# The pool of the large buffer allocated ahead of the constants

## The chip, the core and the metric

The kernel runs on one core of a Trainium2 chip. The metric is the time of one execution on the device, in microseconds, and the median over several executions is what counts. A NeuronCore has a matrix engine (TensorE, PE in the profile, with its weight loads shown apart as PEld), a vector engine (VectorE, DVE), a scalar engine (ScalarE, ACT), a general engine (GpSimd, POOL) and a queue engine (SyncE, SP). Its working memory, SBUF, has 128 partitions; a tile has the same byte address in each of them. The results of matrix products go to another memory, PSUM, in banks of 512 float32 values per partition.

## What is computed

Two graph layers over 4096 nodes with 512 features each, both with a dense 4096 x 4096 adjacency matrix and a layer norm over the sum with their input:

```python
# layer 0
xw = relu(sign(x)) @ sign(w0).T
x1 = layernorm(x + relu(adj @ xw))
# layer 1
node_att = softmax(x1 @ node_w, axis=0)
h = x1 @ edge_w
e = where(adj > 0, h @ h.T, -9e15)
edge_att = softmax(e, axis=1)
out = layernorm(x1 + adj * (node_att * edge_att) @ (x1 @ w1) + bias)
```

All inputs and the output are float32.

## The kernel before

The nodes are handled in 32 blocks of 128 (the partitions) and in 8 groups of 512 (one PSUM bank). The kernel passes through these stages, and TensorE works in all of them:

1. *Signs.* `whole(g)` (L177) loads a part of x transposed, turns it into signs on VectorE and multiplies by the signs of w0 (`bw`). Its result, rows of `xw`, is written by VectorE (L222) and ScalarE. `follow(g)` (L240) multiplies two early row blocks of the adjacency by the rows of `xw` that are there (L246, L247).
2. *First aggregation, adj @ xw.* The loop over `n` (L343 on) takes the other 30 row blocks. For each it loads the block of the transposed adjacency in two halves (`at`, 1 MB each, L358, three buffers), and treats each half in two quarters of 8 column blocks. ScalarE rounds a quarter to the format float32r (`hi`, L363), VectorE takes the difference (`lo`, L365), each with two buffers, and TensorE multiplies hi and lo by the same row of `xw`, adding into one bank (L373, L374): 16 matmuls for a quarter, 64 for a block. hi and lo are the stationary operands (loaded by PEld, 128 x 128), the row `xw[:, kb, :]` of 512 values is the moving operand. Between the quarters VectorE carries the residual, layer norm and node weights of an earlier block (`rest`, L290 on), and the mask of the second layer is made ahead (`premask`, L271 on: a load on the ACT queue, one VectorE instruction, a store on the POOL queue). At each block's end TensorE does four transposes (L333).
3. *h.* `seven` (L90) multiplies with seven products in place of eight; the result is `hT`.
4. *h h^T*, with the masks and row minima (`Single`, `Couple`, L641 and L714), and
5. *the second aggregation and the last product* (`Sums`, L1081, and `Finish`, L1208), with running sums in `sums` and with `w1_s` behind them.

`xw`, `hT` and `over` (of which `sums` and `w1_s` are parts) are one after the other in one buffer of 65,536 bytes per partition: the pool `big`, with one buffer of the tag "large". `xw` and `bw` are float32r, as are hi, lo and `ba`, the signs of x; all other operands of the large products are float32.

The allocator places pools one behind the other in the order in which they are entered, each tile at a multiple of 32 bytes. Ahead of everything stand 16,512 bytes (129 x 128) that the runtime and four small constants use. Before, `const` comes next: `ident` (512 bytes at 16,512), `eps`, `shift`, `node_s`, `nmax`, `gmax`, `node_att`, `nsum` and `gsum`, together 960 bytes. So the large buffer begins at 17,472, which is 136 x 128 + 64. `rows`, `small` and all later pools follow; nearly all their tiles are a multiple of 128 bytes long, so the tiles that hold 512 bytes or more (`at`, `hi`, `lo`, `bw`, `ba`, `warm`, `x1T`, `lent`, `slot`, `lop`, ...) begin at a multiple of 128 plus 64 too. A row of `xw` has 2,048 bytes, so each row of it begins 64 bytes after a multiple of 128.

The lines around the moving operand, and those that allocate it:

```python
    const = ctx.enter_context(tc.tile_pool(name="const", bufs=1))
    big = ctx.enter_context(tc.tile_pool(name="big", bufs=1))
...
    xw = big.tile([P, NB, D], F32R, name="xw", tag="large")
...
                            nc.tensor.matmul(acc, hi[:, c, :], xw[:, kb, :], start=(kb == 0), stop=False)
                            nc.tensor.matmul(acc, lo[:, c, :], xw[:, kb, :], start=False, stop=(kb == NB - 1))
```

Of the kernel before, what the change touches and what calls it, by code (L numbers as in the profile page):

```python
# [29 lines left out]
def kernel(  # L30
# [22 lines left out]
    HD = D // 2  # L53
    QC = HB // 2

    const = ctx.enter_context(tc.tile_pool(name="const", bufs=1))
    big = ctx.enter_context(tc.tile_pool(name="big", bufs=1))
    rows = ctx.enter_context(tc.tile_pool(name="rows", bufs=4))
    small = ctx.enter_context(tc.tile_pool(name="small", bufs=2))
    dram = ctx.enter_context(tc.tile_pool(name="dram", bufs=1, space=bass.MemoryType.DRAM))  # L60
# [98 lines left out]
    with (  # L159
# [110 lines left out]
        bufs = deque([pair[:, 0, :], pair[:, 1, :], single, ends])  # L270
# [1186 lines left out]
```

## Time and profile before

| | |
|---|---|
| median of 5 executions | 1938.6 us (1936.35 to 1938.7) |
| the profiled execution | 1937.62 us |
| its span, first to last instruction | 1935.6 us |
| TensorE's mean granted clock in it | 0.999 of full speed |
| DMA traffic | 508.72 MB, 263 GB/s in the mean |

A row of a group of instructions in the profile has the line, the engine, the operation, the tiles it writes and reads, the shape, the count, then the time in which at least one of the group was busy, the mean duration of one in ns, and the idle time of the engine ahead of them with what ended it. A matmul's duration is counted until its last result, and its end is modelled; matmuls follow one another before the one ahead has ended. How fast they really pass is therefore read from their starts, in the view of instructions in order of time, whose columns are the start in us, the duration in us, engine, line, operation and tiles.

### The profile page before, as it was taken

The page shows a single profiled execution, that of the slowest core. Times are in us where ns is not written, and L with a number is a line of the kernel's source. Part 1 is how long each engine was busy: PE and PEld are TensorE (multiplying, and loading weights), DVE is VectorE, ACT ScalarE, POOL GpSimd, SP SyncE. Part 2 cuts the span into 40 slices and gives each one's busy share as a digit, 9 for nine tenths or more (in the row PEclk, how much of TensorE's full clock was granted, in tenths as well). Part 3 has the DMA queues.
Part 4 walks back from the last instruction along what each step waited for, and adds up shares of the span by engine and source line. Part 5 has one row for each costly group of instructions (what it writes and reads, how often), then busy time and mean ns, then how long its engine had stood idle before and what let it go on. Part 6 is the DMA issues. An engine that isn't in the chain of part 4 may idle for free.

```text
span 1935.6 us, 20238 instructions
## 1 busy us (share of the span) xinstructions
PE 1917.9 (99%) x6742; PEld 1203.5 (62%) x6742; DVE 1389.4 (72%) x2062; ACT 1022.4 (53%) x1614; POOL 291.8 (15%) x413
## 2 busy tenths in 40 slices
PE   9999999999999999999999999999999999999998
PEld 6888888888644445454555444456666666666655
DVE  7766676676765567566664996687869987798747
ACT  5433333333202567576677665546766576757731
POOL 0122122222341101011111111111111110111100
PEclk9999999999999999999999999999999999999999
DMA  8888888887475478577773998777778787877731
GB/s 310 294 325 311 297 317 309 325 311 284 160 266 220 157 259 313 187 276 252 291 309 104 347 343 292 255 273 257 267 263 293 255 274 262 293 274 260 275 109 44
DMA packets 169527, 508.72 MB, mean 263 GB/s; under 512 B 15696, under 2 KB 41040, under 8 KB 161744
## 3 DMA queue, kind: packets, MB, share of 16 engines
q1 hardware_dynamic: 89472, 226.39, 34.9%
q0 software_dynamic: 64688, 239.10, 32.8%
q10 hardware_dynamic: 15264, 41.95, 5.9%
q8 instruction: 53, 0.87, 0.2%
q14 instruction: 50, 0.41, 0.1%
HBM read 385.74 MB, written 121.63 MB: 262 GB/s over the span
## 4 chain that ended last, share of the span: by engine, by line
PE 80%; DVE 10%; issue 4%; DMA 4%; ACT 1%; POOL 0%; POOLq 0%; DVEq 0%; SPq 0%
PE bank L1081 25%; PE seven L714 14%; PE acc L374 11%; PE acc L373 11%; PE pe L641 6%; PE seven L101 4%; PE po L1208 3%; PE pt L603 2%; DVE lent L847 1%; DMA slot<-s_d 1%; DMA lent<-s_d 1%; PE pw L214 1%; PE acc L246 1%; DVE lent L835 1%; PE pt L333 1%
## 5 line engine op out<-in xcount | busy, mean ns | idle before, releaser
L1081 PE MATMUL bank<-lent,lop 128*128 128x512 f32 (+1 forms) x1136 | 420.0, 517 | 0.0
L373 PE MATMUL acc<-xw,hi 128*128 128x512 f32 x960 | 376.4, 392 | 0.0
L374 PE MATMUL acc<-xw,lo 128*128 128x512 f32 x960 | 374.2, 390 | 0.0
L1081 PE MATMUL bank<-slot,lop 128*128 128x256 f32 (+1 forms) x1052 | 356.1, 486 | 1.5 <-DVE slot L862 1.5
L1081 PEld LDWEIGHTS bank<-lent,lop 128*128 128x128 f32 x1136 | 215.7, 190 | 173.9 <-issue 159.0
L1081 PEld LDWEIGHTS bank<-slot,lop 128*128 128x128 f32 x1052 | 199.6, 190 | 135.2 <-issue 116.9
L363 ACT CAST hi<-at 128x1024 fp32r<-128x1024 f32 x120 | 126.4, 1054 | 203.4 <-PE acc L373 148.4
L365 DVE TENSOR_TENSOR lo<-at,hi 128x1024 fp32r<-128x1024 f32 x120 | 146.9, 1224 | 85.0 <-ACT hi L363 85.0
L374 PEld LDWEIGHTS acc<-xw,lo 128*128 128x128 f32 x960 | 180.4, 188 | 37.1 <-DVE lo L365 0.3
L373 PEld LDWEIGHTS acc<-xw,hi 128*128 128x128 f32 x960 | 180.3, 188 | 36.7
L1090 ACT COPY over<-bank 128x512 f32<-128x512 f32 x200 | 114.5, 581 | 108.4 <-PE bank L1081 97.1
L641 PE MATMUL pe<-hT 128*128 128x512 f32 (+3 forms) x384 | 132.1, 486 | 0.0
L574 ACT ACTIVATE line<-line,nmax_c 128x512 f32<-128x512 f32 x160 | 114.8, 725 | 22.5 <-DVE nmax_c L565 22.3
L565 DVE CUSTOM_DVE_ANT_0 line<-lent,slot 128x512 f32<-128x512 bf16 x140 | 90.7, 689 | 48.4 <-ACT slot L651 26.7
L835 DVE CUSTOM_DVE_ANT_1 lent<-lent,line 128x2048 f32<-128x2048 f32 x40 | 91.4, 2286 | 22.6 <-DMA lent<-s_d 13.0
L841 ACT ACTIVATE slot<-slot 128x2048 f32<-128x2048 f32 x36 | 68.9, 1913 | 71.3 <-DMA slot<-in_adj_t_dram 65.4
L838 ACT ACTIVATE lent<-lent 128x2048 f32<-128x2048 f32 x40 | 76.5, 1912 | 54.7 <-DVE lent L835 54.6
L641 PEld LDWEIGHTS pe<-hT 128*128 128x128 f32 x384 | 64.6, 191 | 41.4 <-issue 33.8
L714 PE MATMUL seven<-hT 128*128 128x512 f32 x192 | 89.8, 593 | 0.0
L1053 ACT COPY bank<-over 128x512 f32<-128x512 f32 x144 | 84.9, 596 | 3.0 <-DVE left L973 0.2
L603 PEld LDWEIGHTS pt<-ident,lent 128*128 128x128 f32 x418 | 52.3, 141 | 52.1 <-issue 38.8
L604 ACT COPY slot<-pt 128x512 f32<-128x512 f32 (+3 forms) x123 | 68.4, 559 | 24.0 <-PE pt L603 24.0
(262 smaller groups left out, 2850.7 us busy)
## 6 DMA issues: line engine op xcount, KB each, us to landing
at<-in_adj_t_dram SPq DMA_DIRECT2D x60, 1024.0 KB, 6.8
lop<-lop_d SPq DMA_DIRECT2D x79, 512.0 KB, 4.9
lent<-s_d POOLq DMA_DIRECT2D x39, 1024.0 KB, 7.4
slot<-in_adj_t_dram POOLq DMA_DIRECT2D x38, 1024.0 KB, 7.4
s_d<-slot POOLq DMA_DIRECT2D x30, 1024.0 KB, 6.8
lent<-in_adj_t_dram POOLq DMA_DIRECT2D x26, 1024.0 KB, 7.5
lop<-lop_d SPq DMA_DIRECT2D x99, 256.0 KB, 4.2
lent<-in_adj_dram SPq DMA_DIRECT2D x48, 512.0 KB, 5.7
```

The costliest lines, as they stand in the source:

```text
L363: nc.scalar.copy(hi, aq)
L365: nc.vector.tensor_sub(lo, aq, hi.bitcast(F32))
L373: nc.tensor.matmul(acc, hi[:, c, :], xw[:, kb, :], start=(kb == 0), stop=False)
L374: nc.tensor.matmul(acc, lo[:, c, :], xw[:, kb, :], start=False, stop=(kb == NB - 1))
L565: nc.vector.tensor_tensor_reduce(line, mask, src, -1.0, HUGE, ALU.add, ALU.min, accum_out=nmax_c[:, b, c : c + 1])
L574: nc.scalar.activation(line, line, AF.Exp, bias=nmax_c[:, b, c : c + 1], scale=-1.0, accum_out=sum_c[:, b, c : c + 1])
L603: nc.tensor.transpose(pt[:, j, :], src[:, ts(j, P)], ident)
L641: nc.tensor.matmul(pe[:, lo * P :], hT[:, k, ts(A * BG + i, P)], hT[:, k, (B * BG + lo) * P : (B + 1) * W], start=(k == 0), stop=(k == KD ...
L714: nc.tensor.matmul(ps, left[m][:, k, q, :], right[m][:, k, :], start=(first and k == 0), stop=(k == KD // 2 - 1), skip_group_check=not first,)
L835: pinned[0](nc.vector._custom_dve(TENSOR_ADD_SAT, out=q, in0=q, in1=m, s0=0.0, s1=-HUGE))
L1081: nc.tensor.matmul(ps, lop[:, k, :], rop[:, k, :], start=start, stop=(k == K - 1), skip_group_check=True)
L1090: nc.scalar.copy(self.to(), self.bank[:, : self.w])
```

## The change

The two lines that enter the pools `const` and `big` change places:

```diff
+    big = ctx.enter_context(tc.tile_pool(name="big", bufs=1))
     const = ctx.enter_context(tc.tile_pool(name="const", bufs=1))
-    big = ctx.enter_context(tc.tile_pool(name="big", bufs=1))
     rows = ctx.enter_context(tc.tile_pool(name="rows", bufs=4))
```

In the built program the large buffer (`xw`, `hT`, `over`) then begins at 16,512, a multiple of 128, and the constants stand behind it: `ident` at 82,048 in place of 16,512, both multiples of 128, and the others likewise 65,536 bytes further up. The two pools together are as long as before, so every other tile keeps its address. The instructions of each engine and their order are the same: 3001 rows on TensorE, 2015 on VectorE, 1488 on ScalarE, 389 on GpSimd and 372 on SyncE in both programs.

## The prediction

> **What bounds the kernel now.** I read first the page's chain that ended last, then the busy time by stage, then the starts of single matmuls, and last who waits for whom.
>
> ```profile
> PE 80%; DVE 10%; issue 4%; DMA 4%; ACT 1%; POOL 0%; POOLq 0%; DVEq 0%; SPq 0%
> ...
> L373 PE MATMUL acc<-xw,hi 128*128 128x512 f32 x960 | 376.4, 392 | 0.0
> L374 PE MATMUL acc<-xw,lo 128*128 128x512 f32 x960 | 374.2, 390 | 0.0
> ```
>
> TensorE carries 80% of the chain, and the two groups that read `xw` as moving operand have no idle time ahead of them. They are the first aggregation. The stretches (PE, PEld, DVE, ACT, POOL busy, clock, DMA share, GB/s) show it from 57 to 507 us:
>
> ```profile
> 57.30:507.30 450.00, 449.97 (x2042) 372.29 (x2041) 312.45 (x481) 147.40 (x181) 107.62 (x151) 1.00 0.84 304
> ```
>
> TensorE is busy throughout, VectorE for 312.5 of 450 us (69%), the DMA engines for 84%. So the stage lasts as long as its matmuls, and the question is whether one of them can pass faster. The order of time says how fast they pass. In the middle of a block (start, duration):
>
> ```profile
> 199.63 0.39 PE L373 MATMUL acc<-xw,hi 128*128 128x512 f32 x1
> ...
> 206.89 0.39 PE L373 MATMUL acc<-xw,hi 128*128 128x512 f32 x1
> ```
>
> Between these two starts lie 32 matmuls: 7.26 us / 32 = 226.9 ns each; between most starts of the stage it is 226 or 227 ns. Now a float32 product of 256 columns in the second aggregation, and one of 128 columns, both read the same way:
>
> ```profile
> 1445.72 1.03 PE L1081 MATMUL bank<-slot,lop 128*128 128x256 f32 x4
> 1446.58 1.03 PE L1081 MATMUL bank<-lent,lop 128*128 128x256 f32 x4
> ```
>
> 0.86 us / 4 = 215 ns; over longer runs of starts 215.8. For 128 columns of float32 (the transposes at L603) starts are 109 ns apart. The difference, 106.8 ns for 128 columns, is 0.834 ns a column; with 512 columns of float32 at 429 ns (L1081) the same slope holds: 429 - 215.8 = 213.2 for 256. A float32 column therefore costs 0.833 ns and an instruction some 2.5 ns more. The float32r matmuls take 512 columns in 226.7, so they pass a column in half that, 0.417 ns: 512 x 0.4167 = 213.3, plus 2.5 is 215.8. They miss this by 10.9 ns. In the signs stage the matmuls `bw` x `ba` at L214, float32r too, run at 226 to 227 as well, while a bf16 matmul of 512 columns between two of its kind (L200, from 8.6 us on) is followed by the next after 215 or 216.
>
> The last view, what TensorE waited for in the whole run, has seven entries and these lead (us, times, longest):
>
> ```profile
> PE po L1208 <- DVE xb L1219: 4.3, 6, 1.4
> PE bank L1081 <- DVE slot L862: 1.5, 1, 1.5
> PE seven L101 <- DVE hT L122: 1.3, 1, 1.3
> PE acc L246 <- DVE xw L222: 1.3, 4, 0.6
> ```
>
> None lies in the aggregation. Next to nothing there waits, yet each matmul takes 5% longer than its columns.
>
> **What the Trainium skill says.** *TensorE: Matmul & The Clock Gate*, section "Back-to-back issue gap", gives N / 2.4 + 2.5 ns for an isolated matmul of N columns: 215.8 for 512. The bf16 and two-pass float32 spacings agree (215 to 216 and 429); the float32r spacing of 226.7 doesn't. *SBUF — State Buffer*, "Specifications (TRN2)", gives lines of 16 bytes; both addresses of `xw`, 17,472 and 16,512, are multiples of 16, so by that page nothing changes. Its section "Operand start alignment" is about legality and says that it timed nothing. No page prices a start 64 past a multiple of 128.
>
> **The change part by part.** It removes and adds no instruction and no wait, and moves none past another: the order on each engine, the queues of SP and POOL included, is the same. Only addresses differ. Three things are touched.
>
> *The moving operand of float32r.* The excess is 226.7 - 213.3 = 13.3 ns, or 13.3 / 0.4167 = 32 columns. Thirty-two float32 values are 128 bytes. A row of `xw` has 2,048 bytes: begun at a multiple of 128 it covers 16 pieces of 128 bytes, begun 64 later it touches 17. 17 / 16 x 213.3 = 226.67, and 226 and 227 in the ratio one to two is what the starts show. I infer that the operand is fetched by pieces of 128 bytes, each taking the time of 32 columns, so that a stream of one column per 0.417 ns is held up by the seventeenth; float32 in two passes and bf16 need half the bytes in a given time and don't notice it. That also says why they run at 215.8 and 429 although their operands begin at 64 as well. No matmul before reads float32r from a multiple of 128, so the aligned cost is bounded: above by 226.7 (no gain, unless the alignment itself did harm, for which no view speaks), below by 213.3. I take 215.8, the spacing of the other single-pass matmuls. Gain 10.9 ns.
>
> Main stage: 30 blocks x 64 = 1920 matmuls x 10.9 = 20.9 us. Some 210 of them, just behind the transposes and elsewhere, run at 228 to 236 and 29 at 313 to 319; what holds them I can't see. If these 240 gained nothing, 2.6 us would be lost; I take a third of it, 0.9. Signs stage: 128 matmuls at L246 and L247 x 10.9 = 1.4 us, but there TensorE also waits for VectorE's rows of `xw`, so part of the gain becomes wait; I take 0.6. The 64 at L214 read `bw`, which stays at 64, and gain nothing. Sum: 20.9 - 0.9 + 0.6 = 20.6 us.
>
> *Cover in the stage.* A quarter shrinks from 16 x 226.7 = 3.63 us to 3.45. hi and lo of a quarter are made while the one before is multiplied: 1.05 us on ScalarE (L363) and 1.22 on VectorE (L365), begun when TensorE gives a buffer back. In the steady blocks lo is ready 0.89 to 2.0 us before its first matmul; this lead falls by about 0.17 us and doesn't end. It is what comes next: it would decide if a quarter went below some 2.7 us. Once, at 492 us, lo was late already (0.3 us of wait); there I expect up to 0.2 us more. Transfers: the 84% of DMA time becomes 88%, 304 GB/s about 319. Single slices of a fortieth of this stage move up to 395. The queue of SP waits for buffers, not for bandwidth: 174 us for lo to free `at` (L358), and `at` lands 6.5 us after its issue (9.9 at most) while its three buffers cover 22.5 us, afterwards 21.6. TensorE's weight loads take 188 ns each beside the matmul; at a spacing of 215.8 such loads, of 190 ns, already keep up (L1081, 256 columns). Cover gone would return at most what was gained.
>
> *hT, sums, w1_s and the constants.* Their matmuls are float32 at 429 and 216, without the excess, so nothing is to be had. VectorE and ScalarE read and write them at 0 in place of 64. No instruction of the trace touches a large tile at a multiple of 128, apart from `ident`, whose own start stays one, so this is unmeasured; by the nearest row (L1090, 581 ns for 512 values, some 6 ns, one part in a hundred, up or down) for each, a bound that I set without a row that shows it, on engines with 72% and 53% of the span. I take nothing.
>
> After 507 us the chain is led by TensorE and by waits that begin with its own work (the largest, 1.3 us at 575, hangs from loads and POOL work that starts when the aggregation ends), so the later stages move ahead as a whole; I allow 1.5 us either way. The profiled execution took 1937.6, 1.0 below the median: 1937.6 - 20.6 = 1917.0 for one like it, and 1918.0 from the median. I forecast 1917.
>
> **The rivals.**
>
> *No gain:* the 32 columns belong to float32r (a fixed cost of its weights or its single pass), or the fetch is by 64 bytes or less. For it: all float32r operands of the trace begin at 64, and the skill's line of 16 bytes. Against: float32 with equally large weights has no such excess, and 17 / 16 meets the number exactly. Time 1938, within 1936 to 1940.
>
> *Half the gain:* the matmuls speed up and the stage is then held by lo or by transfers, as each block's worst quarter is. For it: DMA at 84%, and one late lo. Against: the leads above. With half of 20.6 it gives about 1927.
>
> *Slower:* the large buffer now starts at another offset within 128 bytes than the tiles it is combined with, and the instructions of VectorE and ScalarE that take one of each run longer, while the matmuls gain nothing. Place: the copies between banks and `sums` (144 at L1053 and 200 at L1090). At 5% of 590 ns, 344 x 30 ns = 10 us of ScalarE, and half of it exposed gives 1943. It decides only if the exposed loss passes 3.9 us and no gain stands against it. For it: L1053 feeds the banks that TensorE adds into. Against: ScalarE is busy for 410 of the last 686 us and TensorE hardly waits for it.
>
> That the change doesn't do what it says is excluded by the allocation.
>
> **How the numbers follow.** Full gain 0.80, half the gain 0.05, no gain 0.11, slower 0.04. The time is that of the full gain. Its own range goes from all matmuls at 213.3 (2048 x 13.3 = 27 us, 1910) to 215.8 with 240 of them gaining nothing, no help from the signs stage and 1.5 us lost later (1937.6 - 20.9 + 2.6 + 1.5 = 1921). With the half gain and its spread taken in, 1910 to 1929; outside it stay no gain, slower and a little of the rest, under 0.2. A measurement of this kernel tells about 0.2% (3.9 us) from no change: faster 0.85, within it 0.11, slower 0.04.
>
> **What would show it.** Right: in the aggregation starts 215 to 216 ns apart, the rows of L373 and L374 near 380 ns, a block of 64 in about 14.3 us where it was 15.0, L214 still at 226 to 227, L641, L714 and L1081 unchanged, and all after the stage earlier by one amount. Wrong: starts at 226 to 227 again (then it is float32r itself), or starts at 216 and new waits of L373 or L374 for hi, lo or `at` (then the cover was too thin), or longer rows on VectorE and ScalarE where they meet `hT` and `sums`.

## The result, and the profile after

The changed kernel takes 1941.4 us in the median of 24 runs (1936.87 to 1944.52), the kernel before 1937.42 in the median of 44; the ratio is 1.002 with a 95% interval of 1.0014 to 1.0025. It is slower, by 0.14 to 0.25%. The forecast was 1917.

The rows that the prediction started from, from the page of the changed kernel (busy us, mean ns of one, idle time ahead):

```profile
L373 PE MATMUL acc<-xw,hi 128*128 128x512 f32 x960 | 378.2, 394 | 0.0
L374 PE MATMUL acc<-xw,lo 128*128 128x512 f32 x960 | 376.0, 392 | 0.0
```

Before they had 392 and 390 ns. The matmuls on `xw`, which were to gain 10.9 ns each, have lost two. That they lost it in passing, not in waiting, is in the list of what TensorE waited for in the whole run of the changed kernel, here complete:

```profile
PE po L1208 <- DVE xb L1219: 4.9, 7, 1.4
PE bank L1081 <- DVE slot L862: 1.7, 1, 1.7
PE acc L246 <- DVE xw L222: 1.3, 4, 0.6
PE idle L200 <- DVE warm L168: 1.3, 1, 1.3
PE seven L714 <- ACT lent L745: 0.7, 1, 0.7
PE pt L603 <- ACT lent L651: 0.4, 1, 0.4
```

Again nothing of the aggregation is in it. The instructions in order of time (start, duration) give the spacing:

```profile
199.94 0.39 PE L373 MATMUL acc<-xw,hi 128*128 128x512 f32 x1
...
207.26 0.39 PE L373 MATMUL acc<-xw,hi 128*128 128x512 f32 x1
```

32 matmuls lie between: 7.32 us / 32 = 228.8 ns, where the kernel before had 226.7. Most single spacings are 226, 229 or 232, quarter after quarter. A float32r column slot is 0.4167 ns, as worked out in the prediction, so 226.7 is 544 slots for 512 columns and 228.8 is 549.

Where the time came from: summed over the 1920 matmuls of the stage the spacings grow from 439.3 to 442.4 us, by 3.2, and so they do in a second profile of the changed kernel (after_again, below). In this pair of profiles the whole span grew by 2.2 only, since the one wait of 1.3 us ahead of `hT` (L101 for DVE L122) is absent after; that stretch, from the first L101 to the first L641, took 98.7 us before, 96.9 after and 99.0 in a second profile of the changed kernel, so it varies from run to run by some 2 us. The later stages keep their spacings: 429 and 216 ns.

### The profile page after: what moved, and what is told of

Its sections match the earlier page's. It is cut to its first block, busy times and chain, and to the rows that moved or that the text cites. A ratio compares the mean times of both kernels' runs of the same rounds, so it can differ in the third digit from the quotient of the medians.

```text
span 1937.8 us, 20238 instructions
## 1 busy us (share of the span) xinstructions
PE 1920.7 (99%) x6742; PEld 1203.9 (62%) x6742; DVE 1390.1 (72%) x2062; ACT 1022.1 (53%) x1614; POOL 291.9 (15%) x413
## 4 chain that ended last, share of the span: by engine, by line
PE 81%; DVE 9%; issue 5%; DMA 4%; ACT 1%; POOL 0%; SPq 0%; DVEq 0%; POOLq 0%; ACTq 0%
PE bank L1081 24%; PE seven L714 14%; PE acc L374 11%; PE acc L373 11%; PE pe L641 6%; PE seven L101 5%; PE po L1208 3%; PE pt L603 2%; DMA slot<-s_d 1%; DVE lent L847 1%; PE pw L214 1%; PE acc L246 1%; PE pt L333 1%; DVE over L1144 1%; PE acc L247 1%
## 5 line engine op out<-in xcount | busy, mean ns | idle before, releaser
L373 PE MATMUL acc<-xw,hi 128*128 128x512 f32 x960 | 378.2, 394 | 0.0
L374 PE MATMUL acc<-xw,lo 128*128 128x512 f32 x960 | 376.0, 392 | 0.0
L374 PEld LDWEIGHTS acc<-xw,lo 128*128 128x128 f32 x960 | 180.4, 188 | 38.4 <-DVE lo L365 0.3
L373 PEld LDWEIGHTS acc<-xw,hi 128*128 128x128 f32 x960 | 180.4, 188 | 38.2
L641 PE MATMUL pe<-hT 128*128 128x512 f32 (+3 forms) x384 | 132.1, 486 | 0.0
L641 PEld LDWEIGHTS pe<-hT 128*128 128x128 f32 x384 | 64.6, 191 | 41.4 <-issue 33.8
```

The costliest lines, as they stand in the source:

```text
L641: nc.tensor.matmul(pe[:, lo * P :], hT[:, k, ts(A * BG + i, P)], hT[:, k, (B * BG + lo) * P : (B + 1) * W], start=(k == 0), stop=(k == KD ...
```

## The experiments

The theory to test was what the prediction rested on, that the operand is fetched by pieces of 128 bytes and the seventeenth costs 32 slots; against it stood that the 32 slots belong to float32r whatever the address, and that the agreement of the two operands' starts is what the change disturbed.

**Series of matmuls alone (m1_offsets).** A kernel of its own: one line for each series of 48 matmuls, with chosen starts, counted in bytes past a multiple of 128. The line of one series, moving at 0 and stationary at 64:

```diff
+    for i in range(48):
+        nc.tensor.matmul(acc[:128, :512], st[:, i % 16 * 128 + 16 :][:, :128], mov[:, i // 2 % 8 * W + 0 :][:, :512], start=(i == 0), stop=(i == 47))
```

> Products alone, none of the reference's work: series of 48 float32r matmuls with chosen starts of the moving and the stationary operand, then fewer columns of either, then bf16 and float32. Three theories. PIECES (the prediction's, mended: the fetch is by 128 bytes, and the stationary operand counts too): 0 and 0 pass in 215.8 ns, 64 and 64 in 226.7, 256 moving columns at 64 in 9/8 of their time (120 ns), and fewer stationary columns change nothing at 64. WEIGHTS (the 32 extra columns are the weight load, 128 float32 at four a column slot, taken out of the moving stream): about 227 at every offset; with 64 stationary columns 220 (512 + 16 slots), with 32 216 to 217 (512 + 8 slots); 256 moving columns cost 256 + 32 slots, 120 ns; the same stationary tile each time changes nothing. RELATIVE (what counts is whether the two starts agree): 64 and 64 226.7, 0 and 0 226.7, 0 and 64 229, 64 and 0 229. bf16 215.8 and float32 429 whatever their starts.

From its order of time, one line a series (start of the first, time of all). The series are, in order, moving and stationary operand at 64 and 64 (L45), 0 and 64 (L50), 64 and 0 (L55), 0 and 0 (L60), 16 and 0 (L65):

```profile
26.56 8.55 PE L45 MATMUL acc<-mov,st 128*128 128x512 f32 x37
34.95 11.36 PE L50 MATMUL acc<-mov,st 128*128 128x512 f32 x48
46.15 11.37 PE L55 MATMUL acc<-mov,st 128*128 128x512 f32 x48
57.35 11.08 PE L60 MATMUL acc<-mov,st 128*128 128x512 f32 x48
68.27 11.28 PE L65 MATMUL acc<-mov,st 128*128 128x512 f32 x48
```

The starts of neighbouring series give the pace: L50 (46.15 - 34.95) / 48 = 233.3, L55 the same, L60 227.5, and 226.7 once its first seven spacings are past. So with both operands at a multiple of 128 nothing is won: 0 and 0 costs just what 64 and 64 costs. The seventeenth piece doesn't exist as a cost. A mismatch of 64 costs 6.7 ns more here, either way round. Fewer moving columns follow in the same run:

```profile
180.05 8.50 PE L115 MATMUL acc<-mov,st 128*128 128x384 f32 x48
188.39 8.51 PE L119 MATMUL acc<-mov,st 128*128 128x384 f32 x48
196.74 5.92 PE L123 MATMUL acc<-mov,st 128*128 128x256 f32 x48
202.49 5.90 PE L127 MATMUL acc<-mov,st 128*128 128x256 f32 x48
208.23 5.47 PE L131 MATMUL acc<-mov,st 128*128 128x128 f32 x48
213.54 5.52 PE L135 MATMUL acc<-mov,st 128*128 128x128 f32 x48
```

L115, L123 and L131 have both at 64, L119, L127 and L135 both at 0. 384 columns take 173.3 ns = 416 slots, 256 take 120.0 = 288: the columns plus 32, at either start. At 64 the pieces would give the same 32, since one piece more is 32 columns whatever the length; it is the 32 at a start of 0 that they can't give. 128 columns take 111.7 = 268 slots, 140 more than the columns, so the 32 are not a constant for every length; what sets the pace there isn't known. WEIGHTS, which would explain it by the columns of the stationary operand, fell as well: with 64 of them a matmul took 230 ns (220 expected), with 32 of them 231.7 (216 to 217 expected). One stationary tile used again and again ran at 226.7. bf16 passes in 215.8 and float32 in 429.2 at either start. Other differences within 128 (16, 32, 48, 80, 96, 112 bytes) gave 231.1 to 233.3, a moving start 4 bytes off 236.9.

**The kernel with all large tiles at a multiple of 128 (e_all_at_0).**

```diff
-    big = ctx.enter_context(tc.tile_pool(name="big", bufs=1))
+    pad = ctx.enter_context(tc.tile_pool(name="pad", bufs=1)); pad.tile([P, 16], F32, name="pad"); big = ctx.enter_context(tc.tile_pool(name="big", bufs=1))
```

> The kernel before with 64 bytes of padding between the constants and the large buffer, so that xw, hi, lo, bw and all other large tiles begin at a multiple of 128. PIECES (mended): spacing in the aggregation 215.8, the time 20 us below before. WEIGHTS: spacing stays within 226.5 to 229, the time within 0.3% of before. RELATIVE: 226.7, the time of before within 0.1%. MOVING (the start of xw alone sets it, 0 is worse than 64): 229, the time as after the change, 0.2% above before.

Measured: 1936.76 us, ratio to before 0.9996 (0.9988 to 1.0004); spacing 226 and 227. This is the full alignment, more than the prediction asked for, in the kernel itself, and it is worth nothing.

**xw at 64 and the rest at 0 (e_xw64_rest0).** The mismatch the other way round.

```diff
-    big = ctx.enter_context(tc.tile_pool(name="big", bufs=1))
+    big = ctx.enter_context(tc.tile_pool(name="big", bufs=1)); pad = ctx.enter_context(tc.tile_pool(name="pad", bufs=1)); pad.tile([P, 16], F32, name="pad")
```

> The kernel before with 64 bytes of padding behind the large buffer: xw, hT and sums begin at 64 as before, every later tile (hi, lo, bw, at, slot, lop) at a multiple of 128. PIECES (mended): 226.7 with no gain. RELATIVE: 229 in the aggregation, the time 0.2% above before. MOVING: 226.7, the time of before within 0.1%; and L214, whose bw and ba now begin at 0, goes to 229.

Measured: 1947.0 us, ratio 1.0053 (1.0039 to 1.0067), more than double the loss of the change. In its order of time 20 matmuls lie between these two starts:

```profile
206.13 0.40 PE L374 MATMUL acc<-xw,lo 128*128 128x512 f32 x1
...
210.79 0.39 PE L374 MATMUL acc<-xw,lo 128*128 128x512 f32 x1
```

4.66 us / 20 = 233 ns. L214, whose two operands now both stand at 0, has 226 and 227 as its commonest spacings still and none of 229, so MOVING falls; and `xw` at 64 costs 226.7 or 233.3 according to where hi and lo stand. RELATIVE named the direction, but its 229 for both mismatches doesn't hold: 228.8 one way, 233.3 the other.

**The kernels' addresses alone (m2_addresses).** The same kind of kernel, with the byte addresses of xw, hi and lo of each variant and no other engine at work.

> Products alone, none of the reference's work: the aggregation's matmuls with the very addresses of four kernels, with no other engine at work, then some shapes. ADDRESSES (the spacing follows from the starts of the two operands alone): before 226.7, after 229, e_all_at_0 226.7, e_xw64_rest0 233.3, as in the kernels; xw at 16,512 with hi and lo 64 lower 226.7. BESIDE (the other engines' reads or the DMA take part): after and e_xw64_rest0 then come out alike, near 233.3. For the 32 slots: FIXED (each float32r matmul pays 32 slots of 0.4167 ns whatever its columns): 448 columns 200.0, 320 columns 146.7, 64 partitions 226.7, a stationary operand of one repeated column 226.7. READ (the reads of the stationary operand collide with those of the moving one): 448 and 320 the same, but with one repeated column of 4 bytes nearer to 215.8. Four float32r and four bf16 in turn: within the bf16 215.8, within the float32r 226.7.

```profile
46.55 14.67 PE L46 MATMUL acc<-sa,sb 128*128 128x512 f32 x64
61.05 14.83 PE L51 MATMUL acc<-sa,sb 128*128 128x512 f32 x64
75.72 14.69 PE L56 MATMUL acc<-sa,sb 128*128 128x512 f32 x64
90.25 15.10 PE L61 MATMUL acc<-sa,sb 128*128 128x512 f32 x64
105.18 15.03 PE L66 MATMUL acc<-sa,sb 128*128 128x512 f32 x64
120.06 15.09 PE L71 MATMUL acc<-sa,sb 128*128 128x512 f32 x64
```

The lines are before (L46), after (L51), e_all_at_0 (L56), e_xw64_rest0 (L61), then two new ones. Within the first four the spacings are 226.7, 228.9, 226.7 and 233.3, to about a tenth those of the four kernels. So neither the DMA nor VectorE or ScalarE are needed for the effect: ADDRESSES holds for the four kernels. L66 was the surprise: `xw` at 16,512 and hi and lo moved down by 64, all at multiples of 128, yet 232.4 ns, not 226.7. There `xw` is 128 past a multiple of 256 and hi and lo are at one. L71 fits a period of 256 too: `xw` at 16,640, a multiple of 256, with hi and lo 64 past one, takes 233.3 as in e_xw64_rest0.

The shapes that follow in this run were meant to have agreeing starts, both at a multiple of 128. But their stationary operand begins at 217,600, a multiple of 256, and the moving one at 16,512, 128 past one: that is the mismatch of L66, at which the whole matmul takes 232.4. There 320 columns took 146.7 ns, 448 columns 204.2, 64 partitions 233.3, 96 stationary columns 231.7 and one repeated stationary column 231.1 (231.1 at a difference of 64 too). One column is nowhere near 215.8, so READ falls. FIXED can't be judged by these, since its 226.7 and 200.0 were for agreeing starts; it falls by m1_offsets, where with agreeing starts 64 stationary columns took 230 and 128 moving ones 111.7, where 128 + 32 slots would be 66.7. The float32r and bf16 in turn, with the same mismatch, ran at 228 to 232 and 215 to 227 within a type, with extra time at each change of type, and decide nothing.

**The change, mended at hi and lo (e_after_hilo0), and mended as a whole (e_after_pad), beside the change again (after_again).**

```diff
-        tc.tile_pool(name="signs", bufs=2) as sp,
+        tc.tile_pool(name="pad", bufs=1) as pp, tc.tile_pool(name="signs", bufs=2) as sp,
...
-        x1T = wide.tile([P, KD, N], F32, name="x1T")
+        x1T = wide.tile([P, KD, N], F32, name="x1T"); pp.tile([P, 16], F32, name="pad")
```

That is the first, which moves by 64 bytes hi and lo alone, with the few tiles that share their buffers; the second has the same padding behind `const`, which moves every later tile. The third has no edit.

> The changed kernel once more, beside its two mends. All theories: 0.2% above before, spacing 229 in the aggregation.

> The changed kernel with 64 bytes of padding ahead of the pool of hi and lo alone, so that these two begin at a multiple of 128 like xw; everything else keeps the addresses of the changed kernel. OFFSETS (the loss is the mismatch of moving and stationary start in the aggregation): spacing 226.7, the time of before within 0.1%. ELSEWHERE (the loss comes from VectorE and ScalarE where hT and sums at 0 meet tiles at 64, or from the constants): still 0.2% above before.

> The changed kernel with 64 bytes of padding behind the constants, so that every large tile begins at a multiple of 128. OFFSETS: spacing 226.7, the time of before within 0.1%, as e_all_at_0. ELSEWHERE by way of the constants' place: still 0.2% above before.

Measured beside the same runs of before: after_again 1941.27, ratio 1.0017 (1.001 to 1.0024); e_after_hilo0 1938.49, ratio 0.9995 (0.9987 to 1.0003); e_after_pad 1937.56, ratio 0.9995 (0.9987 to 1.0003). In e_after_hilo0:

```profile
286.40 0.39 PE L373 MATMUL acc<-xw,hi 128*128 128x512 f32 x1
...
293.65 0.39 PE L373 MATMUL acc<-xw,hi 128*128 128x512 f32 x1
```

7.25 us / 32 = 226.6. Two tiles moved by 64 bytes take the whole loss away, with `hT`, `sums` and the constants where the change put them. ELSEWHERE falls.

**The law of the difference (m3_law), and the same in the kernel (e_after_hilo128).** Having seen L66, the difference was swept in steps of 64 bytes, with the stationary operand at 0, 64 and 128; and hi and lo of the changed kernel were moved by 192 bytes in place of 64 (the edit is shown against e_after_hilo0):

```diff
-        x1T = wide.tile([P, KD, N], F32, name="x1T"); pp.tile([P, 16], F32, name="pad")
+        x1T = wide.tile([P, KD, N], F32, name="x1T"); pp.tile([P, 48], F32, name="pad")
```

> Products alone, none of the reference's work: 40 float32r matmuls of 512 columns for each difference between the moving and the stationary start, in steps of 64 bytes, each series behind 12 bf16 matmuls so that all begin alike; at the end some differences in turn with no bf16 between. MOD256 (the starts have to agree modulo 256): 226.7 at differences 0, 256, 512 and 768 only, 228 to 234 elsewhere, 232.4 at 128. MOD128: 226.7 at 128, 384 and so on too. MOD512: 226.7 at 0 and 512 only. HISTORY (the spacing depends on the phase in which a series begins): 64 gives one value behind bf16 and another behind a series at 192; without it the same value each time.

> The changed kernel with 192 bytes of padding ahead of the pool of hi and lo, so that xw, hi and lo all begin at multiples of 128, but xw 128 past a multiple of 256 and hi and lo at one. MOD256: spacing 232.4 in the aggregation, 1920 x 5.7 ns = 11 us above before, 0.57%. MOD128: spacing 226.7 and the time of before, as with 64 bytes of padding.

Spacings of the sweep, ns, once each series has settled, by moving minus stationary start modulo 256:

| stationary at | 0 | 64 | 128 | 192 |
|---|---|---|---|---|
| 0 | 226.7 | 228.9 | 232.1 | 233.3 |
| 64 | 226.7 | 228.9 | 232.6 | 233.3 |
| 128 | 226.7 | 228.9 | 233.3 | 233.3 |

With the stationary operand at 0 the moving start went on to 960 in steps of 64, and the row repeats every 256 bytes without a change. A larger piece doesn't save the prediction's idea either: in L313 below both operands begin at a multiple of 1,024, at 226.7. The last series of this run, with no bf16 between them, have differences of 192, 64, 192, 64, 0 and 64:

```profile
358.57 9.48 PE L293 MATMUL acc<-sa,sb 128*128 128x512 f32 x40
367.89 9.32 PE L298 MATMUL acc<-sa,sb 128*128 128x512 f32 x40
377.05 9.50 PE L303 MATMUL acc<-sa,sb 128*128 128x512 f32 x40
386.39 9.32 PE L308 MATMUL acc<-sa,sb 128*128 128x512 f32 x40
395.54 9.24 PE L313 MATMUL acc<-sa,sb 128*128 128x512 f32 x40
404.62 9.34 PE L318 MATMUL acc<-sa,sb 128*128 128x512 f32 x40
```

From start to start 9.32, 9.16, 9.34, 9.15 and 9.08 us for 40: 233, 229, 233.5, 229 and 227 ns. What runs ahead didn't matter here, so HISTORY falls.

In the kernel, e_after_hilo128 took 1946.4 us, ratio 1.0044 (1.0027 to 1.0061):

```profile
291.40 0.39 PE L373 MATMUL acc<-xw,hi 128*128 128x512 f32 x1
...
298.84 0.40 PE L373 MATMUL acc<-xw,hi 128*128 128x512 f32 x1
```

7.44 us / 32 = 232.5 ns, with xw, hi and lo all at multiples of 128. Summed over the stage the spacings are 449.4 us, 10.2 above before (11 expected); MOD256 holds, MOD128 and, by the sweep, MOD512 are out.

**The series that doesn't fit (m4_odd_one).** In m1_offsets moving at 64 and stationary at 0 took 233.3, where the sweep has 228.9 for that difference.

> Products alone, none of the reference's work. In m1_offsets one series with a difference of 64 took 233.3 ns where m3_law has 228.8 for that difference. The same addresses again behind bf16 matmuls, then with fewer slices or rows, then with one operand moved. PLACE (more of the addresses than their difference modulo 256 counts): 233.3 again at those addresses, and 228.8 once one operand is moved by a multiple of 256. PATTERN (which slices follow which): 233.3 with 16 slices, 228.8 with 8 or 1. BEGINNING (the series before it set the phase): 228.8 in all. Differences of 32, 96, 160 and 224: between their neighbours, 227 to 234.

The same addresses with 16 slices and 8 rows gave 233.3 again, in the first float32r series of the run; with 8 slices or one, with one row, or with either operand elsewhere 228.9. PLACE is out. PATTERN and BEGINNING this run alone doesn't separate: the one series that repeats the pattern was also the first, and began before the clock was up (its first ten spacings are 426 ns or more). But in m1_offsets the same pattern gave 233.3 at full clock behind another float32r series, so two different beginnings gave one value, and behind a series at 233.3 the eight slices of m3_law (L298) gave 228.9. That speaks for PATTERN, for 16 slices together with 8 rows, without proving it; the difference of the starts alone doesn't fix the spacing in every case. Differences of 32, 96, 160 and 224 gave 234.3, 233.3, 233.3 and 233.3, so halfway to an agreement nothing is saved.

## Why the prediction was wrong

*What bounds the kernel* was read rightly: the aggregation lasts as long as its matmuls, before and after, and 1.7 ns on each of 1920 of them, 3.2 us together, account for a change that the interval puts between 2.7 and 4.8 us. The excess of 32 column slots at L373 and L374 was read rightly too, from the trace, and it is still there.

*The step that failed* is the one on the moving operand: "17 / 16 x 213.3 = 226.67", and from it "I infer that the operand is fetched by pieces of 128 bytes". The arithmetic met the number to the tenth, and that was luck: the excess of 32 slots happens to be as many columns as 128 bytes hold. With both operands at a multiple of 128, where no seventeenth piece is touched, it is 32 slots as well, with 256, 384 and 512 columns. The term "10.9 ns" for each of 1920 matmuls measures -1.7 ns in the kernel (3.2 us / 1920), and 0 where everything is aligned. The prediction said itself that no matmul before read float32r from a multiple of 128; with one value of the address in the trace, no fit to that value could show an effect of the address. The chance of 0.80 on it was far too high.

*What the bound left out.* The aligned cost was bounded "above by 226.7 (no gain, unless the alignment itself did harm, for which no view speaks)". The harm is what came: the change moved `xw` and left hi and lo, so moving and stationary start, which had both been 64 past a multiple of 256, now differ by 64: `xw` begins 128 past one, hi and lo 64. Undoing the difference at hi and lo alone gives the old time back.

*The rivals.* "No gain" came nearest: the 32 slots stay with the float32r matmul at every start that was tried, though its time, 1936 to 1940, was missed by the mismatch it didn't foresee, and whether weights or single pass cause them isn't shown. "Slower" had the right idea, an offset that no longer agrees with the tiles it is combined with, and the wrong place: it put the loss in VectorE's and ScalarE's copies with `sums`, which e_after_hilo0 excludes; the spacing of TensorE's matmuls follows from the starts of their two operands with no other engine at work. "Half the gain" was not tested by the change, as no quarter became shorter.

*The skill.* *SBUF — State Buffer*, section "Specifications (TRN2)", with its lines of 16 bytes, spoke for no gain from 128, and rightly so as far as that goes; but starts that are all multiples of 16 run at 226.7 or 233.3 here, so that line alone doesn't describe the matmul. N / 2.4 + 2.5 of *TensorE: Matmul & The Clock Gate*, "Back-to-back issue gap", given there for an isolated matmul beside a smaller spacing for a sustained stream, meets the streams of bf16 here (215.8 measured for 512 columns, and none shorter) and not those of float32r, which took N + 32 slots with 256, 384 and 512 columns at agreeing starts, and 268 with 128.

*What stays open:* what the 32 slots are. They don't shrink with fewer stationary columns (230 to 231.7 at agreeing starts) and stay with one stationary tile used again and again (226.7); fewer partitions and one repeated column were only run at a mismatch. Why the period is 256 bytes, why the sign of a difference counts, and why one pattern of slices raises a difference of 64 to 233.3 is open too. No start of the operands that was tried went below 226.7 for 512 columns, so no version was found that beats the kernel before.

## What to carry to other kernels

Where float32r matmuls follow one another and bound a stage, let the moving and the stationary tile start at the same offset modulo 256 bytes: in this kernel the worst mismatch that was tried cost 0.5% of the whole, and an even 128 in both was not enough. An address of one operand is half of a fact; before moving a tile, list the tiles that the same instructions read. And a number that fits a mechanism exactly is no evidence while the trace has one value of the cause: a run with two values of it, ten lines long, would have shown it.

## What the runs showed of the hardware that was not expected

- A float32r matmul of 512, 384 or 256 columns takes its columns plus 32 slots of 0.4167 ns when both starts agree modulo 256 (226.7, 173.3, 120.0 ns); 128 columns took 111.7. At a difference of 128 bytes 512 columns took 232.4, 448 204.2 and 320 146.7, which is 320 + 32 slots still.
- The cost of a mismatch depends on its sign: moving 64 bytes ahead of the stationary start 228.8 to 228.9 ns (233.3 in one pattern of 16 slices and 8 rows), 64 behind it 233.3, 128 apart 232.1 to 233.3. bf16 and two-pass float32 at both starts of 0 and both of 64 were alike, 215.8 and 429.2; their mismatches weren't measured alone.
- Fewer stationary columns made a float32r matmul slower, not faster: 226.7 ns with 128, 230 with 64, 231.7 with 32, all at agreeing starts.
